# A fourth of the aggregation's seven products is split into seven, in eight of its sixteen units

## The chip, the cores and the metric

The kernel runs on one core of a Trainium2 chip. Time is device microseconds of one execution. Of the core's engines the text speaks of TensorE (PE in the profile, with its weight loads as PEld), VectorE (DVE), ScalarE (ACT), GpSimd (POOL, which here issues large loads) and SyncE (SP, which issues the others).

## The reference, cut to what matters

Two graph layers work on 4096 nodes of 512 features. The part that changes is in the second layer.

```python
# layer 0: x = layernorm(x + relu(adj @ (sign_z(x) @ sign(w0).T)))
# layer 1:
node_att = softmax(x @ node_w, axis=0)
h = x @ edge_w
e = where(adj > 0, h @ h.T, NEG_BIG)
edge_att = softmax(e, axis=1)
output = adj * (node_att * edge_att) @ (x @ weight)
x = layernorm(x + output + bias)
```

The product of the 4096x4096 weights `adj * edge_att` with the 4096x512 features, here called the aggregation, is taken before the product with `weight`, and all of it is float32.

## The kernel before, in words

The kernel has these stages in order: layer 0 (up to 507 us), `h` (507 to 605 us), `h @ h.T` (605 to 1079 us), whose scores go to memory with row maxima and sums, then the aggregation from 1081 to 1911 us, and at last the product with `weight` and the layernorm of the last rows.

**The aggregation's units.** The output's 4096 rows stand in four groups, g = 0 to 3, each of two panels of 512 rows (g and g + 4). The 4096 inputs stand in four pairs of panels as well, r = 0 to 3. A unit (`Aggregate(g, r)`) multiplies one pair of input panels with one pair of output panels and adds to the sums of its group. There are 16 units in the order g, then r, so that units 0 to 3 are group 0, units 4 to 7 group 1, and so on. A unit is a 2x2 block product in the Strassen-Winograd form: seven products m = 0 to 6 instead of eight. The seven left operands come from the features, were made once, and are loaded again for each product from `lop_d` (512 KB). The seven right operands of a unit are its four panels of weights, three of them as they are and one overwritten by a difference, and three more differences (`combine`, `right`). Each is a buffer of 1 MB.

**One product.** Unsplit, a product is two sums (`Sums` with h = 0, 1), each of four matmuls that contract 128 rows, 128x128 weights against 512 columns, into one PSUM bank. Split, which products 6, 4 and 3 are in units 4 to 14, it is a 2x2 block product again: seven products of half the size in each direction, each of two matmuls against 256 columns. They are held in four sums: two small products side by side in a bank for (1, 2), (0, 5) and (3, 4), and one alone for (6,). A sum's life is `seed` (line 1037: ScalarE copies the sum so far into a bank, three sums ahead of use; for the first unit of a group the matmul starts afresh, or VectorE zeroes the bank, line 1039), `multiply` (line 1065) and `evict` (line 1074: ScalarE copies the bank back to memory).

**What splitting costs the other engines.** The small right operands need four 128x512 operations of VectorE for each unit and product (`second`, lines 942 to 946). They are issued from `main`, one half after each unsplit sum. The small left operands need four 128x256 operations for each product and r (`lefts`, lines 955 to 958); these are made in group 0, units 0 to 3, and stored to `lop2_d` through ScalarE's queue. A split product then loads 896 KB in four issues of SP (lines 1049 to 1052) into two of four half-tiles of `lopp`; an unsplit one takes one issue and one half-tile. When a group's last unit has run, seven 128x256 operations for each split product (`join_inner`, line 1113) make its four quarters from the seven small sums, two of them after each sum of products.

**The other work beside it.** While a unit multiplies, the panels of the next one are made: the scores are loaded by POOL (line 810), shifted by the row maximum (VectorE, line 823, 128x2048), exponentiated (ScalarE, line 826), the mask is loaded by POOL (line 817), clipped (ScalarE, line 829), and both are multiplied (VectorE, line 835). Then come the four differences of `combine` (lines 848 to 856). A load waits for a free buffer, and a product frees its right operand's buffer when it ends. After a group, in the next group's first units, come its seven joins (`join`, line 1128, 128x1024 each, held back while inner joins are waiting) and its two finishes (`Finish`): small matmuls with `weight` (line 1192), each read from PSUM by VectorE (line 1203) before the same part of the bank is used again, then the layernorm.

**What sets the order.** The code places the side work by shares of a unit's products (`steps`, `between`), and a scheduler of the framework then fixes one order of instructions for each engine when the kernel is built. Each engine runs its list strictly in order, and waits are semaphores.

The memory `sums` holds two groups in turn (`g % 2`), seven products of 128x1024 for each; small sums that don't fit into their own place lie in two further buffers, `extra`, and so do the small right operands.

Of the kernel before, what the change touches and what calls it, by code (L numbers as in the profile page):

```python
# [21 lines left out]
HUGE = 3.4e38  # L22
TWO = 2.0**11
SHIFT = 1.5 * 2.0**34
SPLIT = 6, 4, 3
WARM = 12


# [1 line left out]
def kernel(  # L30
# [13 lines left out]
    nc = tc.nc  # L44
# [3 lines left out]
    W = 512  # L48
    NG = N // W
    BG = W // P  # L50
    HB = NB // 2
    HG = NG // 2
# [746 lines left out]
    class Aggregate:  # L799
# [114 lines left out]
        def order(self, two):  # L914


            ends = (1, 2) if self.r % 2 else (2, 1)
            if self.last:
                order = 1, 0, 5, 2, 6, 4, 3
            elif two:  # L920
                order = ends[0], 6, 5, 4, 0, 3, ends[1]
            else:
                order = ends[0], 0, 4, 6, 5, 3, ends[1]
            for m in order:
                if two and m in SPLIT:
                    for ns in ((1, 2), (6,), (0, 5), (3, 4)):
                        yield Sums(self, m, ns=ns)
                else:

                    more = bool(self.r) and m == order[0]  # L930
                    keep = self.r < HG - 1 and m == order[-1]
                    for h in range(2):
                        yield Sums(self, m, h, more, keep)

        def second(self, m):

            h, w = BG // 2, W // 2
            r = self.right(m)
            (r11, r12), (r21, r22) = [[r[:, k : k + h, c : c + w] for c in (0, w)] for k in (0, h)]
            t2, t3, t4 = (extra[0][:, n, :].rearrange("p (b w) -> p b w", w=w) for n in range(3))  # L940
            self.halves = r11, r21, r22, t4, r12, t2, t3
            nc.vector.tensor_sub(t3, r22, r12)
            nc.vector.tensor_sub(r12, r12, r11)
            yield
            nc.vector.tensor_sub(t2, r22, r12)
            nc.vector.tensor_sub(t4, r21, t2)
            yield
# [20 lines left out]
        def main(self, between, two):  # L968
            uses = deque(u for u in plan if u.unit is self)
            whole = sum(u.work for u in uses)  # L970
            halves = (None for m in [u.m for u in uses if u.ns and u.ns[0] == 1] for _ in self.second(m))
            stores = deque()
            past = 0
            while plan and plan[0].unit is self:
                u = plan.popleft()
                u.seed()
                u.multiply()
                evict()
                written.append(u)
# [12 lines left out]
                between(past / whole, u.work)  # L992
            if stores:
                next(stores.popleft(), None)
# [13 lines left out]
    class Sums:  # L1008
# [5 lines left out]
        def __init__(self, unit, m, h=0, more=False, keep=False, ns=None):  # L1014
# [4 lines left out]
            self.w = W // 2 * len(ns) if ns else W  # L1019
            self.bank = None  # L1020

        def to(self):

            return part(self.unit.g, self.m, self.ns) if self.ns else sums[:, self.unit.g % 2, self.m, self.h, :]

        def seed(self):


            if self.bank is not None or self.more and not kept:
                return  # L1030
            if self.more:
                self.bank = kept.popleft()
                return
            self.bank = banks.popleft()
            if self.unit.r:
                assert self.ns or not any(m == self.m for m, _ in [*inner, *inner_next])
                nc.scalar.copy(self.bank[:, : self.w], self.to())  # L1037
            elif self.w < W:
                nc.vector.memset(self.bank[:, : self.w], 0.0)

        def multiply(self):
# [12 lines left out]
            if self.ns:  # L1054
                products = []
                for k, n in enumerate(self.ns):
                    at = self.lefts[n]
                    lop = lops["high"][:, at - 4] if at > 3 else lops["low"][:, at]
                    products.append((self.bank[:, ts(k, W // 2)], lop, self.unit.halves[n], BG // 2))
            else:  # L1060
                products = [(self.bank, lops["lop"][:, :, ts(self.h, P)], self.unit.right(m), BG)]
            start = not r and self.w == W
            for ps, lop, rop, K in products:
                for k in range(K):
                    nc.tensor.matmul(ps, lop[:, k, :], rop[:, k, :], start=start, stop=(k == K - 1), skip_group_check=True)  # L1065
# [4 lines left out]
        def evict(self):  # L1070
            u = self.unit
            if not self.keep:
                assert u.r or not self.ns or not any(m == self.m for m, _ in [*inner, *inner_next])
# [24 lines left out]
    def join_inner(g, m, n):  # L1098
# [14 lines left out]
        nc.vector.tensor_add(out_, a, b)  # L1113
# [144 lines left out]
    def in_two(n):  # L1258

        return HG <= n < len(blocks) - 1  # L1260
# [85 lines left out]
    for n, u in enumerate(blocks):  # L1346
# [25 lines left out]
        def between(past, work):  # L1372
            while first and first[0][0] <= past + 1e-6:
                first.popleft()[1]()
            for _ in range(2):
                if inner:
                    join_inner(u.g if u.r else (u.g - 1) % HG, *inner.popleft())
            inner.extend(inner_next)
            inner_next.clear()
            owed[0] += work  # L1380
# [59 lines left out]
```

## Time and profile before

| | us |
|---|---|
| median of 9 runs | 1941.94 |
| lowest and highest | 1939.87, 1947.89 |
| profiled execution, its time | 1944.2 |
| profiled execution, its span | 1942.2 |
| aggregation, units 0 to 15 | from 1081.2 to 1910.9 |
| last finishes | 1910.9 to 1942.2 |

The profile's span is the program's own; 2.0 us of the execution's time lie around it. The granted TensorE clock is 0.998. Units begin at 1277.2 (unit 4), 1328.9, 1387.8, 1440.1 (unit 7), 1487.5, 1539.7, 1596.9, 1651.9 (unit 11), 1700.3, 1751.7, 1808.6 and 1857.7 us (unit 15). The duration of a record is longer than the distance from one to the next, because an engine begins an instruction before the one before has fully ended; both are used below, and the text says which.

| group of instructions, units 4 to 14 | count | busy us | mean ns |
|---|---|---|---|
| seeds by ScalarE, 512 wide (line 1037) | 124 | 73.6 | 599 |
| evictions by ScalarE, 512 wide (line 1074) | 170 | 97.8 | 584 |
| evictions by ScalarE, 256 wide (line 1074) | 33 | 12.3 | 374 |
| reads of the finish by VectorE (line 1203) | 78 | 37.0 | 477 |

### The profile page before, as it was taken

The page shows a single profiled execution, that of the slowest core. Times are in us where ns is not written, and L with a number is a line of the kernel's source. Part 1 is how long each engine was busy: PE and PEld are TensorE (multiplying, and loading weights), DVE is VectorE, ACT ScalarE, POOL GpSimd, SP SyncE. Part 2 cuts the span into 40 slices and gives each one's busy share as a digit, 9 for nine tenths or more (in the row PEclk, how much of TensorE's full clock was granted, in tenths as well). Part 3 has the DMA queues.
Part 4 walks back from the last instruction along what each step waited for, and adds up shares of the span by engine and source line. Part 5 has one row for each costly group of instructions (what it writes and reads, how often), then busy time and mean ns, then how long its engine had stood idle before and what let it go on. Part 6 is the DMA issues. An engine that isn't in the chain of part 4 may idle for free.

```text
span 1942.2 us, 20257 instructions
## 1 busy us (share of the span) xinstructions
PE 1920.4 (99%) x6742; PEld 1203.8 (62%) x6742; DVE 1389.4 (72%) x2062; ACT 1022.2 (53%) x1614; POOL 299.9 (15%) x424
## 2 busy tenths in 40 slices
PE   9999999999999999999999999999999999999998
PEld 6888888888644445454555444456666666666655
DVE  7766676676774566577666787587869987798747
ACT  5433333333202567567667566556766577657731
POOL 0122222222341111111112111111011110111100
PEclk9999999999999999999999999999999999999999
DMA  9888888888475478577769998777778777887731
GB/s 310 298 324 312 292 322 310 320 304 292 146 281 206 175 254 318 185 275 257 282 255 326 330 330 301 254 275 254 265 265 293 255 270 263 287 279 253 272 111 44
DMA packets 171751, 517.11 MB, mean 266 GB/s; under 512 B 15872, under 2 KB 41216, under 8 KB 163968
## 3 DMA queue, kind: packets, MB, share of 16 engines
q1 hardware_dynamic: 89472, 226.39, 34.3%
q0 software_dynamic: 66912, 247.49, 34.3%
q10 hardware_dynamic: 15264, 41.95, 5.9%
q8 instruction: 53, 0.87, 0.2%
q14 instruction: 50, 0.41, 0.1%
HBM read 389.94 MB, written 125.83 MB: 266 GB/s over the span
## 4 chain that ended last, share of the span: by engine, by line
PE 79%; issue 6%; DMA 6%; DVE 6%; ACT 2%; POOL 1%; POOLq 0%; SPq 0%; DVEq 0%; ACTq 0%
PE bank L1065 30%; PE seven L702 12%; PE acc L374 11%; PE acc L373 11%; PE seven L101 4%; PE po L1192 3%; PE pe L633 2%; PE pt L603 2%; DMA s_d<-slot 2%; DMA slot<-s_d 2%; DMA lop<-lop_d 1%; ACT line L574 1%; PE pw L214 1%; PE acc L246 1%; DMA lent<-in_adj_t_dram 1%
## 5 line engine op out<-in xcount | busy, mean ns | idle before, releaser
L1065 PE MATMUL bank<-lent,lop 128*128 128x512 f32 (+1 forms) x1292 | 426.1, 481 | 0.0
L373 PE MATMUL acc<-xw,hi 128*128 128x512 f32 x960 | 376.4, 392 | 0.0
L374 PE MATMUL acc<-xw,lo 128*128 128x512 f32 x960 | 374.2, 390 | 0.0
L1065 PE MATMUL bank<-slot,lop 128*128 128x512 f32 (+1 forms) x896 | 347.1, 535 | 0.7 <-ACT bank L1037 0.7
L1065 PEld LDWEIGHTS bank<-lent,lop 128*128 128x128 f32 x1292 | 246.0, 191 | 154.9 <-issue 133.2
L1065 PEld LDWEIGHTS bank<-slot,lop 128*128 128x128 f32 x896 | 170.0, 190 | 153.8 <-issue 142.3
L363 ACT CAST hi<-at 128x1024 fp32r<-128x1024 f32 x120 | 126.4, 1054 | 203.4 <-PE acc L373 148.4
L365 DVE TENSOR_TENSOR lo<-at,hi 128x1024 fp32r<-128x1024 f32 x120 | 148.0, 1234 | 84.3 <-ACT hi L363 84.3
L374 PEld LDWEIGHTS acc<-xw,lo 128*128 128x128 f32 x960 | 180.4, 188 | 37.0 <-DVE lo L365 0.3
L373 PEld LDWEIGHTS acc<-xw,hi 128*128 128x128 f32 x960 | 180.3, 188 | 36.7
L1074 ACT COPY over<-bank 128x512 f32<-128x512 f32 x200 | 114.8, 581 | 121.0 <-PE bank L1065 111.7
L633 PE MATMUL pe<-hT 128*128 128x512 f32 (+3 forms) x384 | 132.1, 486 | 0.0
L574 ACT ACTIVATE line<-line,nmax_c 128x512 f32<-128x512 f32 x160 | 114.8, 725 | 20.9 <-DVE nmax_c L565 20.8
L565 DVE CUSTOM_DVE_ANT_0 line<-lent,slot 128x512 f32<-128x512 bf16 x144 | 93.1, 688 | 45.2 <-ACT slot L643 22.4
L829 ACT ACTIVATE slot<-slot 128x2048 f32<-128x2048 f32 x40 | 76.5, 1912 | 71.6 <-DMA slot<-in_adj_t_dram 71.4
L823 DVE CUSTOM_DVE_ANT_1 slot<-slot,line 128x2048 f32<-128x2048 f32 x36 | 82.4, 2288 | 36.3 <-DMA slot<-s_d 35.9
L826 ACT ACTIVATE slot<-slot 128x2048 f32<-128x2048 f32 x36 | 68.9, 1913 | 43.0 <-DVE slot L823 42.5
L633 PEld LDWEIGHTS pe<-hT 128*128 128x128 f32 x384 | 64.6, 191 | 41.4 <-issue 33.8
L702 PE MATMUL seven<-hT 128*128 128x512 f32 x192 | 89.8, 593 | 0.0
L1037 ACT COPY bank<-over 128x512 f32<-128x512 f32 x144 | 84.8, 596 | 3.2 <-ACT over L1074 0.4
L603 PEld LDWEIGHTS pt<-ident,lent 128*128 128x128 f32 x412 | 51.2, 141 | 55.2 <-issue 38.8
L604 ACT COPY slot<-pt 128x512 f32<-128x512 f32 (+3 forms) x126 | 69.5, 554 | 27.8 <-PE pt L603 24.0
(260 smaller groups left out, 2864.6 us busy)
## 6 DMA issues: line engine op xcount, KB each, us to landing
at<-in_adj_t_dram SPq DMA_DIRECT2D x60, 1024.0 KB, 6.8
slot<-in_adj_t_dram POOLq DMA_DIRECT2D x42, 1024.0 KB, 6.8
lop<-lop_d SPq DMA_DIRECT2D x79, 512.0 KB, 4.9
slot<-s_d POOLq DMA_DIRECT2D x36, 1024.0 KB, 7.8
s_d<-slot POOLq DMA_DIRECT2D x33, 1024.0 KB, 6.8
lent<-s_d POOLq DMA_DIRECT2D x28, 1024.0 KB, 7.7
lop<-lop_d SPq DMA_DIRECT2D x99, 256.0 KB, 4.4
lent<-in_adj_dram SPq DMA_DIRECT2D x48, 512.0 KB, 5.1
```

What stands on the lines that cost most here:

```text
L363: nc.scalar.copy(hi, aq)
L365: nc.vector.tensor_sub(lo, aq, hi.bitcast(F32))
L373: nc.tensor.matmul(acc, hi[:, c, :], xw[:, kb, :], start=(kb == 0), stop=False)
L374: nc.tensor.matmul(acc, lo[:, c, :], xw[:, kb, :], start=False, stop=(kb == NB - 1))
L565: nc.vector.tensor_tensor_reduce(line, mask, src, -1.0, HUGE, ALU.add, ALU.min, accum_out=nmax_c[:, b, c : c + 1])
L574: nc.scalar.activation(line, line, AF.Exp, bias=nmax_c[:, b, c : c + 1], scale=-1.0, accum_out=sum_c[:, b, c : c + 1])
L603: nc.tensor.transpose(pt[:, j, :], src[:, ts(j, P)], ident)
L633: nc.tensor.matmul(pe[:, lo * P :], hT[:, k, ts(A * BG + i, P)], hT[:, k, (B * BG + lo) * P : (B + 1) * W], start=(k == 0), stop=(k == KD ...
L702: nc.tensor.matmul(ps, left[m][:, k, q, :], right[m][:, k, :], start=(first and k == 0), stop=(k == KD // 2 - 1), skip_group_check=not first,)
L1037: nc.scalar.copy(self.bank[:, : self.w], self.to())
L1065: nc.tensor.matmul(ps, lop[:, k, :], rop[:, k, :], start=start, stop=(k == K - 1), skip_group_check=True)
L1074: nc.scalar.copy(self.to(), self.bank[:, : self.w])
```

## The change

Product 5 is split as well, in the units with two levels that are not the first of their group: units 5, 6, 7, 9, 10, 11, 13 and 14. The first unit of each group still computes it whole, into the sum's own place.

- In these eight units the order of products is now first end, 6, 0, 4, 5, 3, second end, where it was first end, 6, 5, 4, 0, 3, second end. Products 4, 5 and 3, all split, now follow one another.
- The small sums of product 5 lie in the place of product 0 of the other group, and its small right operands in that of products 5 and 6, which are free once the other group's joins are done.
- In the second unit of a group the sums (0, 5) and (6,) begin afresh, since the first unit left a whole product. One operation then subtracts one quarter of that from another (n = 7 in `join_inner`), so that the seven later additions give the right quarters.
- `second` is now issued after the six sums of unsplit products and two of product 5's own, by counts of 1, 1, 2, 2, 1, 1. Those before product 3 are issued while product 5 runs.
- The left operands of product 5 are made in units 1, 2 and 3 and stored with the others.
- `join_inner` makes 28 operations for a group, and one more, where it made 21.

```diff
-SPLIT = 6, 4, 3
+SPLIT = 6, 4, 3, 5
+LATER = 5
@@ order
+            elif two and not self.r:
+                order = ends[0], 6, 5, 4, 0, 3, ends[1]
             elif two:
-                order = ends[0], 6, 5, 4, 0, 3, ends[1]
+                order = ends[0], 6, 0, 4, 5, 3, ends[1]
...
-                if two and m in SPLIT:
+                if two and m in SPLIT and (self.r or m != LATER):
                     for ns in ((1, 2), (6,), (0, 5), (3, 4)):
@@ second
-            t2, t3, t4 = (extra[0][:, n, :].rearrange("p (b w) -> p b w", w=w) for n in range(3))
-            self.halves = r11, r21, r22, t4, r12, t2, t3
+            buf = sums[:, (self.g + 1) % 2, 5:7].rearrange("p m h w -> p (m h) w") if m == LATER else extra[0]
+            t2, t3, t4 = (buf[:, n, :].rearrange("p (b w) -> p b w", w=w) for n in range(3))
+            self.halves[m] = r11, r21, r22, t4, r12, t2, t3
@@ main
-            halves = (None for m in [u.m for u in uses if u.ns and u.ns[0] == 1] for _ in self.second(m))
+            self.halves = {}
+            halves = deque(x for u in uses if u.ns and u.begin for x in [self.second(u.m)] * 2)
+            counts = deque((1, 1, 2, 2, 1, 1) if self.r else (1,) * 6)
...
-                if not u.ns:
-                    next(halves, None)
+                if counts and (not u.ns or u.m == LATER and u.ns[0] in (1, 6)):
+                    for _ in range(min(counts.popleft(), len(halves))):
+                        next(halves.popleft())
...
-                    if not self.g and u.m in SPLIT:
+                    if not self.g and u.m in SPLIT and (self.r or u.m != LATER):
                         stores.append(self.lefts(u.m, lops["lop"]))
@@ Sums
+            self.new = not unit.r or bool(ns) and m == LATER and unit.r == 1 and ns[0] in (0, 6)
...
-            if self.unit.r:
-                assert self.ns or not any(m == self.m for m, _ in [*inner, *inner_next])
+            if not self.new:
+                assert not any(m == self.m for m, *_ in [*inner, *inner_next])
                 nc.scalar.copy(self.bank[:, : self.w], self.to())
...
-            start = not r and self.w == W
+            start = self.new and self.w == W
...
-                inner_next.extend((self.m, n) for n in range(7))
+                inner_next.extend((self.m, n, u.g) for n in range(7))
+            if self.end and self.m == LATER and not u.r and in_two(blocks.index(u)):
+                inner_next.append((self.m, 7, u.g))
@@ part
+        if m == LATER:
+            return sums[:, (g + 1) % 2, 0].rearrange("p h w -> p (h w)")[:, slice(0, 2 * w) if len(ns) == 2 else slice(2 * w, 3 * w)]
@@ join_inner
+        if n == 7:
+            nc.vector.tensor_sub(c12, c12, c22)
+            return
```

More of the change, by code (lines that the diff above doesn't have):

```diff
@@ L1058, in multiply @@
                     lop = lops["high"][:, at - 4] if at > 3 else lops["low"][:, at]
-                    products.append((self.bank[:, ts(k, W // 2)], lop, self.unit.halves[n], BG // 2))
+                    products.append((self.bank[:, ts(k, W // 2)], lop, self.unit.halves[m][n], BG // 2))
             else:
                 products = [(self.bank, lops["lop"][:, :, ts(self.h, P)], self.unit.right(m), BG)]
-            start = not r and self.w == W
+            start = self.new and self.w == W
             for ps, lop, rop, K in products:
@@ L1072, in evict @@
             if not self.keep:
-                assert u.r or not self.ns or not any(m == self.m for m, _ in [*inner, *inner_next])
+                assert u.r or not any(m == self.m or m == LATER and not self.m for m, *_ in [*inner, *inner_next])
                 nc.scalar.copy(self.to(), self.bank[:, : self.w])
@@ L1096, with join_inner @@
     inner, inner_next = deque(), deque()
[L1098 removed]
+    def join_inner(m, n, g):
         w = W // 2
         (c11, c12), (c21, c22) = ((x[:, :w], x[:, w:]) for x in (sums[:, g % 2, m, h, :] for h in range(2)))
+        if n == 7:
+            nc.vector.tensor_sub(c12, c12, c22)
+            return
         both = part(g, m, (0, 5))
@@ L1376, in between @@
                 if inner:
-                    join_inner(u.g if u.r else (u.g - 1) % HG, *inner.popleft())
+                    join_inner(*inner.popleft())
             inner.extend(inner_next)
```

## The prediction

> **What bounds the kernel.** I read the page's head and chain first, then TensorE's own order of time, then who kept TensorE waiting, then each engine's load unit by unit.
>
> ```profile
> span 1942.2 us, 20257 instructions
> PE 1920.4 (99%) x6742; PEld 1203.8 (62%) x6742; DVE 1389.4 (72%) x2062; ACT 1022.2 (53%) x1614; POOL 299.9 (15%) x424
> ...
> PE 79%; issue 6%; DMA 6%; DVE 6%; ACT 2%; POOL 1%; POOLq 0%; SPq 0%; DVEq 0%; ACTq 0%
> ```
>
> TensorE (PE) is busy throughout and carries the chain. A busy TensorE can still hide slack, so its pace has to be read where the change works. This is unit 7 of the aggregation in order of time (start, length, count):
>
> ```profile
> 1448.80 19.12 PE L1065 MATMUL bank<-lent,lop 128*128 128x256 f32 x72
> 1467.75 7.03 PE L1065 MATMUL bank<-slot,lop 128*128 128x512 f32 x16
> 1474.62 6.21 PE L1065 MATMUL bank<-lent,lop 128*128 128x256 f32 x28
> ```
>
> One matmul leaves two records. The second line is one whole product: 16 records in 7.03 us, the last of which counts for its full 592 ns, so the pitch is (7.03 - 0.592) / 15 = 0.429 us. The third is one split product: (6.21 - 0.379) / 27 = 0.216 us. Half the columns take 1.5 ns more than half the time; weight loads, 190 ns each, fit under both. (The first line merges products of both kinds.) The busy sums of the page's groups give 0.442 and 0.235, because the modelled end of one record overlaps the next group; I don't use them.
>
> What TensorE waited for between 1277 and 1858 us, units 4 to 14 (total us, times, longest), is little:
>
> ```profile
> PE po L1192 <- DVE xb L1203: 4.8, 7, 1.1
> PE bank L1065 <- ACT bank L1037: 0.7, 1, 0.7
> ```
>
> So whatever shortens the matmul stream there shortens the kernel, as long as the other engines keep up. Units 7, 8, 11 and 12 by engine (stretch, sum, then busy time of PE, PEld, DVE, ACT, POOL):
>
> ```profile
> 1440.10:1487.50 47.40, 47.40 (x165) 29.91 (x164) 38.20 (x42) 34.28 (x48) 5.99 (x8) 1.00 0.84 296
> 1487.50:1539.70 52.20, 51.05 (x173) 32.59 (x172) 52.07 (x54) 27.91 (x32) 6.73 (x9) 1.00 0.77 267
> ...
> 1651.90:1700.30 48.40, 47.74 (x166) 29.87 (x165) 37.16 (x36) 33.95 (x46) 5.98 (x8) 1.00 0.83 288
> 1700.30:1751.70 51.40, 51.03 (x174) 32.49 (x173) 51.24 (x53) 26.71 (x32) 6.41 (x9) 1.00 0.75 259
> ```
>
> VectorE (DVE) is full in units 8 and 12, where a group's joins fall, and about 80% full in the units before. Its lateness is what TensorE waits for at the end of unit 8:
>
> ```profile
> 1535.41 2.29 DVE L823 CUSTOM_DVE_ANT_1 lent<-lent,line 128x2048 f32<-128x2048 f32 x1
> 1537.62 0.68 DVE L945 TENSOR_TENSOR lent<-slot 128x512 f32<-128x512 f32 x1
> 1538.22 0.48 DVE L1203 SCALAR_TENSOR_TENSOR xb<-po,f,xb 128x256 f32<-128x256 f32 x1
> ...
> 1538.75 1.13 PE L1192 MATMUL po<-over 128*128 128x256 f32 x4 [1.15 <-DVE xb L1203]
> ```
>
> **The change, part by part.** Eight units (5, 6, 7, 9, 10, 11, 13, 14) compute product 5 split.
>
> *Matmuls.* Each of the eight loses 8 matmuls of 512 columns (16 records) and gains 14 of 256 (28 records): 16 x 0.429 = 6.86 us becomes 28 x 0.216 = 6.05 us, 0.82 us saved, 6.5 us for eight. All of it is on the bounding engine. [...] This stage's rows already hold both widths at 0.216 and 0.429 us and decide for the saving.
>
> *VectorE.* A 128x512 operation shows 0.68 us but follows the next at 0.605 us when VectorE is full, a 128x256 one shows 0.42 us and follows at 0.335 us (three joins of line 1113 at 1492.87 take 1.09 us: (1.09 - 0.42) / 2). Added:
> - The right-hand combinations: 4 per unit, 32 x 0.605 = 19.4 us.
> - The inner joins: 7 for each of three groups and one subtraction for each, 24 x 0.335 = 8.0 us, and three zeroings of 0.2 us.
> - The left-hand combinations in units 1, 2 and 3: 12 x 0.335 = 4.0 us, and 6 stores issued from ScalarE's queue. Those units have 7.0, 25.2 and 6.9 us of VectorE idle each, and TensorE doesn't wait there: 0 (at worst, uncovered, 1.3 us in each of two).
>
> Units 4 to 14 have 101 us of VectorE idle in 580, so the average is no problem. The places are. Units with r = 1 or 2 get 2.4 us against 7.8 to 15.7 us of idle: hidden, except where an eviction of the finish (line 1203) comes out later behind other work. Of the present evictions many reach TensorE with 0.1 to 3 us to spare. I put 0.5 us on those of units 4 to 6; those of units 9, 10, 13 and 14 follow waits for panels (6.2 us of VectorE idle in unit 9 alone) that swallow the lag.
>
> At the full unit 8 I counted. In unit 7 VectorE idles 8.84 us before line 763, until TensorE's matmul of line 772 is done; the built order puts product 5's four combinations ahead of that, into the idle time. From line 763 to the eviction at 1538.22 the built order has eight more 128x256 operations and two fewer 128x512: 8 x 0.335 - 2 x 0.605 = +1.5 us. TensorE arrives 0.8 us earlier. Its wait there grows by 2.3 us, and the next one (0.83 us, at 1544) is then already served: +1.5 us. In units 11 to 13 the same count gives 1 to 2 us, but 3.25 us of VectorE's idle time, a wait for a panel at 1679, lies in that stretch: +0.5 us. Together +2.5 us. Bounds: -4.8 (the new order removes today's waits too) and +11.7 (the rival below).
>
> *ScalarE.* 13 copies of 0.58 us and 13 of 0.38 us more, 12.5 us in all or 1.6 us per unit, in units where it is busy 68 to 75%. Seeds are written three sums ahead. The one wait today, 0.7 us at 1696.7, comes from a clip (line 829) that waits 4.61 us for its mask load and stands ahead of the last product's second seed; in the built order of units 7 and 11 that clip comes after both seeds. I take -0.7. Bounds: -0.7, and +4.5, if in each of units 7, 11 and 14 an operation of 1.9 us gets in front of a seed that has about 0.4 us to spare, as one had at 1679.6.
>
> *Loads.* A split product loads 896 KB in four issues instead of 512 KB in one. SP issues 24 more at 0.3 to 0.5 us each; SP itself mostly waits for buffers. With 4, 5 and 3 now in a row and four buffers in turn, the second half-tile of 5 and of 3 can be issued one split product (6.05 us) before its product, and is used 12 records (2.6 us) into it: 8.6 us of lead, where it was 11.5. Such loads land in 4.4 us in the median, the slowest in 8.7 to 9.3. I take +0.3 us, between 0 and +3 (0.7 us short on half of the eight). POOL's panel loads wait for buffers that a product frees; 0 and 5 change places, but a buffer still comes free at the end of each product and the second still lasts 6.86 us, so they keep their times: 0.
>
> Sum: -6.5 + 2.5 - 0.7 + 0.3 = -4.4 us. The profiled execution took 1944.2 us (span 1942.2 and 2.0 around it), 2.3 above the median of 1941.94; it would become 1939.8, and the median 1937.5.
>
> **Rivals.** A difference under 0.2%, 3.9 us, is about what this kernel's times (1939.87 to 1947.89) can't tell from none. The saving stays above that while new waits are under 2.6 us, and the kernel is slower by it from 10.4 us of new waits.
>
> 1. VectorE takes the gain at its full units. In the middle: its lag passes on at half its size in the two full units and at some tight evictions, new waits of about 4.5 us, 1939.9. For: slack of 0.1 to 3 us before many evictions. Against: panel waits that take up lag. Slower: nothing is absorbed. All that a unit with r = 3 and the next one gain (2.4 + 2.3 + 0.3 us) and the 0.8 us by which TensorE comes earlier pass on, 5.9 us at each of the two full units: 11.7 - 6.5 = +5.2, 1947.1. Against: the count above, +1.5 instead of 5.
> 2. ScalarE holds back seeds in the run 4, 5, 3: +4.5 instead of -0.7, and the rest as forecast: 1942.7. For: split products need 4.1 us of copies in 6.05 us, and exponentials of 1.9 us come between. Against: most seeds are 3 us or more ahead, and the clip's new place.
> 3. Late left operands: +3 instead of +0.3, 1940.2. DMA is 75 to 84% busy already.
> 4. The narrow matmuls don't hold 0.216 us with operands in the sums' memory, say 0.235: 224 x 0.019 = 4.3 us back, 1941.8; at 0.245, with the waits, it is slower. Nothing in the rows speaks for it.
> 5. Today's waits (5.5 us) vanish too: -12, 1930.
>
> **Chances.** Forecast 0.45, within 1935.4 (no new waits) to 1938.0. Rival 5, in part, 0.06. Rival 1 in the middle 0.22, slower 0.08. Rival 2 0.09, rival 3 0.06, rival 4 0.04, of which 0.03 slower. So faster 0.51, same 0.38, slower 0.11. The range runs from 1934 to 1944: it leaves out most of rival 5, the slower end of 1 and 4, and little else.
>
> **What would show it.** Right: 1136 records of 512 columns and 1148 of 256 under the product line at 0.429 and 0.216; units 5, 6, 7 and so on shorter by 0.8 us where nothing waits; waits of TensorE for line 1203's evictions near 7 us in total, most of the growth at the end of units 8 and 12; none for seeds in unit 11. Wrong: those waits well over 10 us (rival 1), a wait for the seed copies of several us (rival 2), for left operands (rival 3), or split pitches above 0.216 (rival 4). The forecast errs most easily on the new order of VectorE's work, which decides which eviction stands behind which 2.2 us operation.

## The result, and the profile after

The changed kernel takes 1951.03 us (median of 10 runs, 1947.02 to 1956.09), where the kernel before takes 1942.80 us (median of 32, 1939.87 to 1947.89). The ratio is 1.0042, with a 95% interval from 1.0033 to 1.005: slower by 8.2 us, outside the predicted range of 1934 to 1944. The profiled execution took 1948.07 us, 3.9 us more than the profiled one of before: that one lay 1.4 us above its median and this one 3.0 us below, so the pair of traces holds less than half of the difference.

Line numbers in the rows are each kernel's own; lines 1212, 1223, 1076, 824 and 857 of the changed kernel are 1192, 1203, 1065, 823 and 856 of the kernel before. First the head of the page of the changed kernel, to be held against that of before:

```profile
span 1946.3 us, 20611 instructions
PE 1916.3 (98%) x6838; PEld 1221.8 (63%) x6838; DVE 1422.5 (73%) x2133; ACT 1030.9 (53%) x1640; POOL 300.7 (15%) x424
```

TensorE is busy for 4.1 us less, VectorE for 33.1 us more. Now TensorE in order of time (start, length, count), in unit 7: a split product and a whole one.

```profile
1449.12 6.21 PE L1076 MATMUL bank<-lent,lop 128*128 128x256 f32 x28
1455.16 7.03 PE L1076 MATMUL bank<-slot,lop 128*128 128x512 f32 x16
```

Both lengths are those of before, to the digit. The line of the products has 1136 records of 512 columns and 1148 of 256, as forecast. The saving of the matmuls is therefore there, and unit 7 shows it whole: 46.5 us where it had 47.4. What TensorE waited for in units 4 to 14 (1275 to 1862 us; total us, times, longest):

```profile
PE po L1212 <- DVE xb L1223: 9.7, 8, 2.9
PE bank L1076 <- ACT bank L1048: 3.0, 2, 2.4
PE bank L1076 <- DVE lent L950: 1.2, 1, 1.2
PE bank L1076 <- DMA lop<-lop_d: 0.8, 1, 0.8
```

14.7 us, where it was 5.5. Units 7, 8, 11 and 12 by engine (stretch, sum, busy time of PE, PEld, DVE, ACT, POOL, then clock, DMA share, GB/s):

```profile
1440.50:1487.00 46.50, 46.50 (x177) 32.15 (x176) 38.05 (x45) 34.64 (x51) 5.99 (x8) 1.00 0.87 302
1487.00:1541.20 54.20, 51.30 (x174) 32.55 (x173) 53.56 (x57) 28.23 (x34) 6.73 (x9) 1.00 0.77 269
1653.40:1700.60 47.20, 47.02 (x177) 31.98 (x176) 37.99 (x42) 35.20 (x51) 5.98 (x8) 1.00 0.87 298
1700.60:1754.70 54.10, 50.45 (x169) 31.75 (x168) 51.81 (x57) 28.04 (x34) 6.36 (x9) 1.00 0.73 258
```

Units 7 and 11 are shorter by 0.9 and 1.2 us, units 8 and 12 longer by 2.0 and 2.7. VectorE (third busy time) fills unit 8 still, and not quite unit 12. The wait at the end of unit 8, in order of time:

```profile
1534.27 0.48 DVE L1223 SCALAR_TENSOR_TENSOR xb<-po,f,xb 128x256 f32<-128x256 f32 x1
1534.66 2.28 DVE L857 TENSOR_TENSOR lent<-slot,lent 128x2048 f32<-128x2048 f32 x1
1536.86 0.69 DVE L947 TENSOR_TENSOR lent<-slot 128x512 f32<-128x512 f32 x1
1537.46 2.29 DVE L824 CUSTOM_DVE_ANT_1 lent<-lent,line 128x2048 f32<-128x2048 f32 x1
1539.67 0.48 DVE L1223 SCALAR_TENSOR_TENSOR xb<-po,f,xb 128x256 f32<-128x256 f32 x1
...
1540.20 1.13 PE L1212 MATMUL po<-over 128*128 128x256 f32 x4 [2.90 <-DVE xb L1223]
...
1745.16 1.13 PE L1212 MATMUL po<-line,line 128*128 128x256 f32 x4 [2.48 <-DVE xb L1223]
```

Between the two evictions stand two operations of 2.28 us, the last `combine` and a shift. Before, only the shift stood there (the prediction shows its row, at 1535.41), and the `combine`, then line 856, came ahead of the first eviction:

```profile
1532.22 2.28 DVE L856 TENSOR_TENSOR slot<-lent,lent 128x2048 f32<-128x2048 f32 x1
1534.42 0.48 DVE L1203 SCALAR_TENSOR_TENSOR xb<-po,f,xb 128x256 f32<-128x256 f32 x1
```

VectorE is never idle here; it does other things first. The last line of the rows of after is the like wait at the end of unit 12. The longest wait that isn't for an eviction is in unit 5. A row of VectorE, ScalarE's rows and then TensorE's:

```profile
1358.53 2.29 DVE L824 CUSTOM_DVE_ANT_1 slot<-slot,line 128x2048 f32<-128x2048 f32 x1 [2.33 <-DMA slot<-s_d]
...
1360.86 1.91 ACT L827 ACTIVATE slot<-slot 128x2048 f32<-128x2048 f32 x1 [3.73 <-DVE slot L824]
...
1363.14 1.92 ACT L830 ACTIVATE lent<-lent 128x2048 f32<-128x2048 f32 x1
1365.07 1.28 ACT L1256 ACT_TABLE_LOAD   x1
...
1367.51 0.60 ACT L1048 COPY bank<-over 128x512 f32<-128x512 f32 x1
...
1368.16 3.57 PE L1076 MATMUL bank<-lent,lop 128*128 128x256 f32 x8 [2.41 <-ACT bank L1048]
```

ScalarE waited 3.73 us for a shift of VectorE, and that shift had waited 2.33 us for its scores to land. Then 6.6 us of ScalarE's own work, an exponential and a clip among it, stood ahead of the seed. The last line has a second cost: 8 records of 256 columns take 3.57 us, where 8 such records take 1.89 us elsewhere in this trace. They run at half the clock: the granted clock is 0.50 from 1368.0 to 1371.4 us (more below).

The profiled execution adds up so. From the distances between records, stalls in units 4 to 14 (whatever is beyond the pitch: waits, smaller gaps, and records at half the clock) grew from 7.8 to 21.3 us, +13.5 (units 4 to 6: +4.0; 7 and 8: +2.0; 9, 10 and 14: +2.8; 11 to 13: +4.7); the matmuls save 6.5; the aggregation began 2.5 us earlier than in the execution shown of before, and what follows unit 15 was 0.7 us shorter. 13.5 - 6.5 - 2.5 - 0.7 = +3.8, against 3.9 measured. The earlier start doesn't come from the change: over the twenty traces of this text the aggregation begins anywhere between 1078.7 and 1083.7 us. The aggregation alone, from its first product to the end of its last, took 837.1 us instead of 829.9.

### The profile page after: what moved, and what is told of

Same layout as the page of the kernel before. It is cut to its first block, busy times and chain, and to the rows that moved or that the text cites. A ratio compares the mean times of both kernels' runs of the same rounds, so it can differ in the third digit from the quotient of the medians.

```text
span 1946.3 us, 20611 instructions
## 1 busy us (share of the span) xinstructions
PE 1916.3 (98%) x6838; PEld 1221.8 (63%) x6838; DVE 1422.5 (73%) x2133; ACT 1030.9 (53%) x1640; POOL 300.7 (15%) x424
## 5 line engine op out<-in xcount | busy, mean ns | idle before, releaser
L1076 PE MATMUL bank<-lent,lop 128*128 128x256 f32 (+1 forms) x1212 | 400.4, 479 | 5.4 <-ACT bank L1048 3.0
L1076 PEld LDWEIGHTS bank<-lent,lop 128*128 128x128 f32 x1212 | 230.8, 191 | 148.3 <-issue 122.4
L1076 PEld LDWEIGHTS bank<-slot,lop 128*128 128x128 f32 x976 | 185.0, 190 | 142.6 <-issue 127.0
L1085 ACT COPY over<-bank 128x512 f32<-128x512 f32 x216 | 121.3, 573 | 91.6 <-PE bank L1076 80.9
L1048 ACT COPY bank<-over 128x512 f32<-128x512 f32 (+1 forms) x154 | 89.8, 590 | 5.4 <-DVE over L1133 2.6
L827 ACT ACTIVATE slot<-slot 128x2048 f32<-128x2048 f32 x37 | 70.8, 1913 | 39.4 <-DVE slot L824 38.1
L830 ACT ACTIVATE slot<-slot 128x2048 f32<-128x2048 f32 x28 | 53.6, 1913 | 64.0 <-DMA slot<-in_adj_t_dram 64.0
L830 ACT ACTIVATE lent<-lent 128x2048 f32<-128x2048 f32 x32 | 61.1, 1911 | 49.1 <-DMA lent<-in_adj_t_dram 46.8
```

The source lines that it names most:

```text
L830: nc.scalar.activation(self.a[n], self.a[n], AF.Relu)
```

## The experiments

All times are medians beside runs of the kernel before on the same chip; the difference to those runs is given, for the changed kernel +8.2. The ratios are taken over whole sets of runs and need not be those of the medians.

### VectorE's added work, or the order of products

```diff
# e1_no_joins
-            if self.end and self.ns and (u.r == HG - 1 ...
+            if self.end and self.ns and self.m != LATER and (u.r == HG - 1 ...
-                inner_next.append((self.m, 7, u.g))
# e2_no_right_sums, in second()
+            if m == LATER:
+                self.halves[m] = r11, r21, r22, r11, r12, r21, r22
+                yield
+                yield
+                return
# e3_neither: both
# e4_order_alone, in the kernel before
+            elif two and self.r:
+                order = ends[0], 6, 0, 4, 5, 3, ends[1]
```

> Leaves out of the changed kernel the seven inner joins of product 5 in three groups and the three subtractions that go with them (24 operations of 128x256 on VectorE, 8 us by the 0.335 us row), so product 5 is not put together at the end. Matmuls, copies, loads and the order of products stay. Theory V (VectorE's added work makes it late, and TensorE waits for it, directly at line 1223's evictions and indirectly through ScalarE's seeds): the waits at 1540 and 1745 us of the changed kernel's profile (3.06 and 2.64 us), which lie behind these joins, fall to 1.5 us or less each, and the time to 1945 to 1948, against 1951.0 of the changed kernel. Theory O (the new order, with three split products in a row, makes ScalarE and the loads late, whatever VectorE does): 1950 to 1952, with the waits of units 5 and 9 unchanged.

> Leaves out of the changed kernel product 5's four right-hand combinations in each of eight units (32 operations of 128x512 on VectorE, 19.4 us); the raw quarters of the right-hand panel are used in their place, so product 5's value is not the reference's. The joins stay. Theory V: most of the lateness in units 5, 9 and 13 goes, the seed wait of 2.58 us at 1368 with it, and the wait at 1745 shrinks; 1943 to 1946. If the joins alone were the cause, 1949 to 1951. Theory O: 1950 to 1952.

> Leaves out both the joins and the subtractions of product 5 and its right-hand combinations, so that VectorE has the load of the kernel before but for the left-hand combinations of three early units; TensorE's matmuls, ScalarE's copies, the loads and the order of products are the changed kernel's. The output is not the reference's. Theory V: what is left is the saving of the matmuls, 6.5 us: 1935 to 1938, and TensorE's waits in units 4 to 14 are about 5 us as before. Theory O: these waits remain at some 12 us, and the time is 1947 to 1951.

> The kernel before with the changed kernel's order of products alone (0 third, 5 fifth) in the units after the first of each group; product 5 is not split. Theory V: as before, 1941 to 1944. Theory O: slower by most of what the change lost besides its saving of 6.5 us, so 1947 to 1955.

| | median us | to before | ratio, 95% interval |
|---|---|---|---|
| e1, without joins | 1950.78 | +8.3 | 1.0036 (1.0023 to 1.0049) |
| e2, without right-hand combinations | 1950.27 | +7.8 | 1.0042 (1.0030 to 1.0054) |
| e3, without both | 1948.18 | +5.7 | 1.0031 (1.0020 to 1.0042) |
| e4, new order alone | 1946.24 | +3.8 | 1.0015 (1.0005 to 1.0025) |

Theory V falls as it stood: 27 us of VectorE's work taken out bring 2.5 us, and the saving of 6.5 us stays away. Theory O is nearer: e1, e2 and e3 lie in its ranges, though for the order alone it began at 1947, a little too high. Yet most of the waits are still for VectorE. The order alone, which adds no operation to any engine, has this at the end of unit 8:

```profile
1536.44 0.47 DVE L1205 SCALAR_TENSOR_TENSOR xb<-po,f,xb 128x256 f32<-128x256 f32 x1
...
1538.88 2.28 DVE L823 CUSTOM_DVE_ANT_1 lent<-lent,line 128x2048 f32<-128x2048 f32 x1
1541.09 0.48 DVE L1205 SCALAR_TENSOR_TENSOR xb<-po,f,xb 128x256 f32<-128x256 f32 x1
...
1541.62 2.07 PE L1194 MATMUL po<-over 128*128 128x256 f32 x4 [3.25 <-DVE xb L1205]
```

Up to this eviction VectorE has one shift more since the start of the unit than in the kernel before (six, where it has five): the scheduler wrote VectorE's list anew, and other rows of the trace show the same (one 128x2048 operation moved from unit 9 to unit 8, a shift from unit 12 to 13). The wait is 3.25 us where it was 1.15, and the four records behind it take 2.07 us instead of 1.13, at about half the pace.

### Long operations, pinned shifts, and an exchange of two split products

```diff
# f1_halved (changed kernel) and f4_before_halved: shift, weigh and combine
-            pinned[0](nc.vector._custom_dve(TENSOR_ADD_SAT, out=q, in0=q, in1=m, ...))
+            for k in (slice(0, 2), slice(2, 4)):
+                pinned[0](nc.vector._custom_dve(TENSOR_ADD_SAT, out=q[:, k], in0=q[:, k], in1=m[:, k], ...))
# f2_pinned_shift (changed kernel)
-            pinned[0](nc.vector._custom_dve(TENSOR_ADD_SAT, ...
+            tc.keep_in_program_order(nc.vector._custom_dve(TENSOR_ADD_SAT, ...
# f3_swap_6_3_4 (kernel before)
-                order = ends[0], 6, 5, 4, 0, 3, ends[1]
+                order = ends[0], 6, 5, 3, 0, 4, ends[1]
```

> The changed kernel with VectorE's long operations (shift, mask product and the four differences of the panels, 128x2048, 2.28 us each) issued as two halves of 1.14 us; nothing is left out, and some 0.03 us are added for each. Theory Q (the loss is that an eviction or a combination which TensorE waits for stands behind a 2.28 us operation in VectorE's list): the waits of TensorE for line 1223's evictions halve, from 9.7 to about 5 us in units 4 to 14, and the time falls to 1944 to 1948. Theory S (the loss lies in what a split product asks of ScalarE and of the loads, and VectorE only shows it): 1950 to 1953.

> The changed kernel with each shift (line 824) held behind everything that the code issued on VectorE before it, where the scheduler lets the shifts of the unit after next go ahead of the finish's evictions. Nothing is left out. Theory Q: the waits at the ends of units 8 and 12 shrink to 1 us or less, unless the shifts come too late for their unit; 1943 to 1948. Theory S: 1950 to 1953.

> The kernel before with two split products, 4 and 3, in each other's place in the two-level units; the work of every engine and the places of split and unsplit products stay as they were. It is an edit with no cost of its own. Theory R (every edit makes the scheduler write VectorE's list anew, the list of before has fewer long operations ahead of evictions than a typical one, and the loss of 3.8 us that the new order alone showed is of that kind): 1944 to 1948, with waits at other places. Theory P (the place of product 5 behind 4 is what costs): 1941 to 1944, as before.

> The kernel before with the same halving of VectorE's long operations as in the changed kernel's run of this set. Theory Q: its 5.5 us of waits in units 4 to 14 fall to about 3, so 1939 to 1942. Theory S: as before or slower by the added 0.03 us for each, 1942 to 1945.

Measured: f1 1951.05 (+8.7), f2 1947.70 (+5.4, its runs from 1940.13 to 1959.19), f3 1943.12 (+0.8; ratio 1.0003, 0.9994 to 1.0012), f4 1948.96 (+6.6; 1.0030, 1.0018 to 1.0042). Theory Q in its simple form falls: halves don't help, the changed kernel still waits 11.0 us for evictions in the profiled run, and the kernel before loses 6.6 us by them. Theory S has f1 in its range, but not f4 (1942 to 1945). Pinning the shifts helps by some 3 us, with a large spread. Theory R in its widest form falls too: the exchange of 3 and 4 costs nothing, as theory P had it. In its trace VectorE has, unit by unit, the same numbers of operations of each kind as before in units 4 to 13. So not every edit costs. The new order alone (e4), which does cost, moved long operations between units; that the moves are its cause is not shown.

### Copies, loads, and the joins on GpSimd

```diff
# g1_no_copies: on top of e3
+            self.new = not unit.r or bool(ns) and m == LATER
...
+                if self.m != LATER or not self.ns:
                     nc.scalar.copy(self.to(), self.bank[:, : self.w])
# g2_raw_left: on top of e3
+            if self.begin and (not self.ns or m == LATER):
                 lops["lop"] = lopp.tile([P, BG, HD], F32, name="lop")
# g3_both: both
# g4_pool_joins (changed kernel, complete)
-            todo.extend(lambda g=u.g, n=n: join(g, n, nc.vector) for n in range(7))
+            todo.extend(lambda g=u.g, n=n: join(g, n, nc.gpsimd) for n in range(7))
```

> The run without joins and right-hand combinations, in which also ScalarE's copies of product 5's small sums are left out (32 evictions and 26 seeds; the sums start afresh in each of the eight units), so that ScalarE has less to do than in the kernel before. Matmuls, loads and the order of products stay. That run took 1948.2 us where the saving of the matmuls alone would give 1936. Theory A (ScalarE's copies, dense in the run of products 4, 5, 3, hold TensorE back): 1938 to 1942. Theory L (the loads of the small left operands do): 1947 to 1950. Theory N (neither: the units' other work sets the pace once TensorE is faster, by whatever stands ahead in VectorE's list): 1945 to 1949.

> The run without joins and right-hand combinations, in which also product 5's small left operands are not loaded or made: one load of 512 KB as for an unsplit product, and its raw quarters used for the seven small matmul pairs. Copies stay. Theory L: 1938 to 1942. Theory A: 1947 to 1950. Theory N: 1945 to 1949.

> Both of this set's omissions in one kernel: of the split of product 5 only the matmuls, and the new order of products, remain. Theories A and L: 1937 to 1940, the order's own loss of 3.8 us and the saving of 6.5 us. Theory N: 1943 to 1947; the saving of the matmuls turns into waits even with nothing added.

> The changed kernel, complete, with the seven outer joins of a group (128x1024, 1.14 us each on VectorE) done by GpSimd, which takes longer for each but is idle 85% of the time. VectorE loses 8 us of work in units 4 and 5, 8 and 9, 12 and 13, and the finishes start later. Theory V (VectorE's fullness in units 8 and 12 is what TensorE waits for): the waits at their ends go, 1944 to 1948. Theory Q (what stands directly ahead of an eviction decides, not the load): 1948 to 1953, with waits at other places.

Measured: g1 1952.65 (+9.9), g2 1945.01 (+2.3), g3 1949.62 (+6.9), g4 2000.70 (+58). Theory A falls: without 58 of ScalarE's copies the kernel is 4.2 us slower than with them (+9.9 against +5.7). In g1's trace no wait for a seed is left in units 4 to 14, but 10.4 us of waits for evictions and 2.7 us for right-hand combinations are. Leaving out the loads gains about 3 us in both pairs (e3 to g2, g1 to g3), less than theory L wants, and what is left in g3, the matmuls and the order, is still slower than before. That is theory N, though it was too low for g1 and g3, which lie 3.7 and 2.6 us above its ranges. Theories V and Q both missed g4. The GpSimd joins took 3.3 us each, where VectorE takes 1.2, and the products that wait for the joins' memory came 6.2 to 6.6 us late in units 4, 8 and 12; that run says little of VectorE's fullness. Three kernels that differ in these omissions show one wait at the end of unit 8. First e3, then g1, TensorE in order of time:

```profile
1543.91 1.42 PE L1215 MATMUL po<-over 128*128 128x256 f32 x4 [2.40 <-DVE xb L1226]
```

```profile
1544.13 1.13 PE L1216 MATMUL po<-over 128*128 128x256 f32 x4 [2.40 <-DVE xb L1227]
```

2.40 us in both (and in g3), with ScalarE's copies and without. In all three the same four operations of VectorE, two shifts of 2.28 us and two combinations of 0.68 us, stand between the two evictions there, without a gap: the length of the wait comes from what stands in VectorE's list.

### Room on VectorE, the old order, a slower pace

```diff
# h1_after_no_outer, h2_before_no_outer
-            todo.extend(lambda g=u.g, n=n: join(g, n, nc.vector) for n in range(7))
+            todo.extend([lambda: None] * 7)
# h3_split_old_order (changed kernel)
-                order = ends[0], 6, 0, 4, 5, 3, ends[1]
+                order = ends[0], 6, 5, 4, 0, 3, ends[1]
-            counts = deque((1, 1, 2, 2, 1, 1) if self.r else (1,) * 6)
+            counts = deque((2, 2, 1, 1, 1, 1) if self.r else (1,) * 6)
# h4_after_pace65 (changed kernel)
-            while owed[0] >= 6:
-                owed[0] -= 6
+            while owed[0] >= 6.5:
+                owed[0] -= 6.5
```

> The changed kernel without the seven outer joins of the first three groups (21 operations of 128x1024 on VectorE, 1.14 us each, 8 us in each of units 4, 8 and 12 with their neighbours); seven empty steps keep their place in time. The output leaves those joins out. Theory 1 (no room on VectorE in units 8 and 12): TensorE's waits at the ends of these units go, and this kernel is as fast as the kernel before without the same joins or faster, up to the 6.5 us of the matmuls: 1936 to 1941. Theory 2 (the order of products): its loss of some 4 us stays, 1945 to 1949.

> The kernel before without the same outer joins, as the base for the run above. Theory 1: its few waits in units 8, 9 and 12 (about 4 us) go, 1938 to 1941. Theory 2: 1940 to 1943.

> The changed kernel with product 5 split but left in its old place, third, ahead of 4 and 0, in all two-level units; its right-hand combinations come during the first product. Complete. Theory 2: about 4 us faster than the changed kernel, 1944 to 1948. Theory 1: VectorE's work in units 7, 8, 11 and 12 is the same, so 1948 to 1954.

> The changed kernel with the steps of joins and finishes issued after every 6.5 units of matmul work instead of 6, so that the same work of VectorE lies over more units. Complete. Theory 1: less of it in units 8 and 12, shorter waits there, 1944 to 1949. Theory 2: the order's loss stays, 1949 to 1952.

Measured: h1 1958.86 (+16.0; ratio 1.0088, 1.0073 to 1.0102), h2 1950.12 (+7.2; 1.0037, 1.0025 to 1.0049), h3 1951.77 (+8.9), h4 1952.40 (+9.5). Both theories fall. Without 24 us of VectorE's work both kernels are slower by 7 to 8 us. The trace of h2, VectorE and then TensorE at the end of unit 12, shows how that can be:

```profile
1721.88 2.29 DVE L823 CUSTOM_DVE_ANT_1 slot<-slot,line 128x2048 f32<-128x2048 f32 x1 [3.67 <-DMA slot<-s_d]
...
1729.13 2.29 DVE L835 TENSOR_TENSOR lent<-lent,slot 128x2048 f32<-128x2048 f32 x1 [1.98 <-ACT lent L826]
...
1735.04 2.28 DVE L835 TENSOR_TENSOR slot<-slot,slot 128x2048 f32<-128x2048 f32 x1
...
1737.85 2.28 DVE L850 TENSOR_TENSOR lent<-lent,slot 128x2048 f32<-128x2048 f32 x1
...
1740.65 2.28 DVE L853 TENSOR_TENSOR lent<-lent,lent 128x2048 f32<-128x2048 f32 x1
1742.85 0.48 DVE L1203 SCALAR_TENSOR_TENSOR xb<-po,f,xb 128x256 f32<-128x256 f32 x1
...
1734.67 1.03 PE L1192 MATMUL po<-over 128*128 128x256 f32 x4
...
1743.38 2.07 PE L1192 MATMUL po<-line,line 128*128 128x256 f32 x4 [4.27 <-DVE xb L1203]
```

The sums that the eviction at 1742.85 reads were done by 1735.7. VectorE had idled in this unit, for a panel and for ScalarE, because its list has those operations first; then three operations of 2.28 us (lines 835 at 1735.04, 850 and 853) stood ahead of the eviction, and TensorE waited 4.27 us. With less to do, VectorE had a worse order. That the change costs 8.7 us in this pair too (h1 to h2) speaks against the joins as its cause. The old order (h3) brings no gain with the split, and the slower pace none.

### The same lists, other loads

```diff
# i1_after_packed, i2_before_packed: left operands kept as [P, 7, 2, BG, P]
-                nc.sync.dma_start(low[:, :2].rearrange("p n b f -> p (n b) f"), raw[:, :, :P])
+                nc.sync.dma_start(low[:, :2].rearrange("p n b f -> p (n b) f"), raw[:, 0])
...
-                nc.sync.dma_start(high[:, 2], raw[:, BG // 2 :, P:])
+                nc.sync.dma_start(high[:, 2], raw[:, 1, BG // 2 :])
```

> The changed kernel, complete, with the left operands kept in memory with the two halves of a product's 256 columns apart, so that a small left operand is read in pieces of 1 and 2 KB instead of 512 bytes. Bytes, issues and the order of instructions on every engine in the aggregation stay; the packets of 512 bytes (9.5% of the 16 engines' time in units 4 to 14 of the changed kernel) go, and the same 15.7 MB take about 7.5%. Layer 0 writes the operands in shorter pieces. Theory D (the loads' share of the DMA engines decides how late the panels are, and with them VectorE): waits shrink, 1944 to 1948. Theory R (the lists alone): 1949 to 1953.

> The kernel before with the same layout of the left operands. Theory D: a gain as well, smaller, since its units leave more room on the DMA engines: 1939 to 1942. Theory R: 1941 to 1944.

Measured: i1 1952.25 (+10.7; ratio 1.0048, 1.0036 to 1.0060), i2 1942.27 (+0.7; 1.0003, 0.9994 to 1.0012). Theory D falls, theory R holds, though the test was weaker than written: the packets of 512 bytes moved 17.9 bytes per ns and DMA engine, those of 1 and 2 KB some 21, so that they took 9.4% of the engines' time and their successors 8.2%, not 7.5%. The lists of TensorE, VectorE and ScalarE are the same, instruction for instruction, in i1 and the changed kernel, and in i2 and the kernel before. What the pair does show is how closely the waits belong to the lists. TensorE's waits in units 4 to 14 of i1, and its two long waits for evictions in order of time:

```profile
PE po L1212 <- DVE xb L1223: 12.7, 9, 2.9
PE bank L1076 <- ACT bank L1048: 2.1, 1, 2.1
PE bank L1076 <- DVE lent L950: 1.7, 1, 1.7
```

```profile
1541.05 1.13 PE L1212 MATMUL po<-over 128*128 128x256 f32 x4 [2.90 <-DVE xb L1223]
...
1746.38 1.13 PE L1212 MATMUL po<-line,line 128*128 128x256 f32 x4 [2.48 <-DVE xb L1223]
```

2.90 and 2.48 us, as in the changed kernel, to the digit, in another execution with other packets. The seed wait of unit 5 is there too (2.1 us). These two waits are no accident of one run: the order of instructions brought them both times.

**All traces together.** TensorE's time in units 4 to 14 can be parted in each of the twenty traces into stalls, counted from the pitch as above, and the rest. The rest is 572.5 us in each of the six kernels that compute product 5 whole, and 564 to 568 us in the fourteen that split it: the saving of the matmuls is in all of them. The stalls are 6 to 15 us in the six and 16 to 28 us in the fourteen (71 with the joins on GpSimd), whatever else was left out or moved. In g3, which keeps only the matmuls of the split and the new order, they are 20 us, where the order alone (e4) has 10. In each of the fourteen the stalls thus grew by at least 8 us over the kernel before, which has 8, and that is more than the matmuls save. A single unlucky list doesn't account for it.

## Why the prediction was wrong

**The premise.** "Whatever shortens the matmul stream there shortens the kernel" rested on the chain of the whole span, 79% TensorE, and on how little TensorE waited. Read for units 4 to 14 alone, the chain of the kernel before says something else. Its pieces in order of time (start, length, what), shown only from 1620 to 1740 us:

```profile
1620.54 7.55 DMA lent<-in_adj_t_dram
1628.12 1.92 ACT lent L829
...
1645.55 0.74 POOL lent L810
...
1668.26 10.88 DMA slot<-s_d
...
1679.25 2.29 DVE slot L823
...
1736.79 2.29 DVE slot L848
1739.07 0.41 DVE xb L1203
1739.52 1.13 PE po L1192 x4
```

From 1613.4 to 1739.5 us, the end of unit 10, unit 11 and most of unit 12, the chain has no TensorE in it. It goes through the making of the panels: a buffer comes free, POOL issues a load, the load takes 7.6 to 10.9 us, ScalarE and VectorE work on it, and VectorE reaches the eviction that TensorE waits for (0.37 us, at 1739.5). Added up over units 4 to 14, TensorE has 377 of the chain's 581 us (65%); with the new order alone (e4) 276 of 583, without VectorE's added work (e3) 187 of 588, without the loads as well (g2) 174 of 587. (The rest is VectorE, loads, and time for which the profile shows no releaser, much of it ahead of POOL's issues. Releasers are inferred, so these are readings and not measurements.) The reading that fits is that two chains of nearly the same length ran side by side; the change shortened one, and the other set the pace. The shares don't prove it, for they don't follow the loss: TensorE has 307 and 333 us of the chain in f3 and i2, which lose nothing, but 352 in g3, 357 in h2 and 374 in f4, which lose 6.6 to 7.2 us. One wait of 0.37 us is enough to give 126 us of the chain to other engines, at a time when TensorE was busy almost throughout. In the changed kernel the chain could be followed back to 1722 us only; it begins there in the making of the panels:

```profile
1722.43 10.69 DMA lent<-in_adj_t_dram
1733.14 1.92 ACT lent L830
1735.08 2.29 DVE slot L836
```

Step by step:

- **Matmuls, -6.5: right.** Pitches, lengths and counts as forecast; rival 4 is out.
- **VectorE, +2.5: this is the step that failed.** In its place the profile has +6.1 us: waits for evictions grew by 4.9 us (4.8 to 9.7), and one for a right-hand combination (1.2) came. They are larger than the term although most of VectorE's added work is hidden. For unit 8, the one counted instruction by instruction, +1.5 was forecast together with the next wait, and stalls in units 8 and 9 grew by 1.8. But 0.5 us each for units 4 to 6 and 11 to 13, and nothing for 10 and 14, became 4.0, 4.7 and 3.0 us of stalls by all causes. The term had been worked out as a sum of added work. The runs show that leaving the work out hardly helps (27 us of work, 2.5 us of time), so a sum of work was the wrong measure. At the ends of units 8 and 12 the rows show what made the waits: which operations stand between two evictions in VectorE's list, which is new with nearly every edit. That this order makes the whole loss is argued, not shown; in unit 5 it began with a load that landed late.
- **ScalarE, -0.7: wrong in sign, within its bounds.** Waits for seeds grew from 0.7 to 3.0 us, 2.4 of them in unit 5. Rival 2 had it right that exponentials would get in front of a seed, but not what follows: they were late because a shift came late from VectorE, and without ScalarE's added copies (g1) the waits for seeds are gone and the time is longer all the same.
- **Loads, +0.3: near, as far as TensorE waits for them** (0.8 us). Their part in the panels' chain was left out: without product 5's small loads the time falls by 3 us in both pairs, with lists that changed as well. Which of the two it is stays open.
- **The clock was not in the sum.** The granted clock over all runs averages 0.9987 in the kernel before (88 runs) and 0.9975 in the changed one (11). TensorE is busy for 98% of the span, so the lost share is about the lost time, an estimate: 0.0013 x 1940 = 2.5 and 0.0025 x 1949 = 4.9 us. The difference, 2.4 us, is nearly a third of the 8.2. It isn't a cause beside the waits: in unit 5 the clock of 0.50 comes behind a wait of 2.41 us, and the table below has half pace behind all 11 stalls of 3.2 us and more.
- **Rival 1** came closest, in its slower end: TensorE's gain turned into waits, 1947.1 at a chance of 0.08. Its half-way middle, 1939.9, had 0.22. New waits of 10.4 us, the point that I named for slower, were nearly reached by the profile's waits (14.7 - 5.5 = 9.2 us) and passed by the stalls (+13.5 us), which hold smaller gaps and the records at half the clock as well. That the waits come without VectorE's added work (e3, g3) the rival did not have.

**What stays open.** No run holds the split together with VectorE's list of before, so what makes the stalls is not settled: that they come with the split is shown for fourteen lists, that the shorter matmul stream meets a second chain is the reading that fits best. As it is the change costs 8.2 us; with three edits made to both kernels it cost 2.1 (halved operations, 8.7 against 6.6), 8.7 (no outer joins) and 10.0 us (packed loads, 10.7 against 0.7): it never paid. No version tried is faster than the kernel before.

## What to carry to other kernels

Read the chain for the stage that the change touches, not for the span: where it leaves the bounding engine for long stretches, a second chain of about the same length may be there, and a saving on the first may turn into waits (here 6.5 us of matmuls saved, and 13.5 us more of stalls). How long those stretches are didn't tell how much was lost here. Where a scheduler writes each engine's list, cost an edit by the new list at every place where an engine is full, and don't expect less work to mean less time (with 24 us less of VectorE's work both kernels were slower by 7 to 8 us). Several short waits can cost less than one long one of the same sum: 2 of 68 stalls of 1 to 2 us were followed by half pace, and all 11 of 3.2 us and more (next section).

## What the runs showed of the hardware

A long wait of TensorE can cost more than its length: behind the 2.41 us of unit 5 in the changed kernel eight records took 1.68 us longer (3.57 us, not 1.89). In all 20 traces the stalls of 1 us and more after 1200 us were counted, with the pace of the matmuls behind them (a stall is the distance to the next record beyond the pitch):

| stall | how many | followed by half pace |
|---|---|---|
| 1 to 2 us | 68 | 2, both closely behind a stall of over 6 us |
| 2.0 to 3.1 us | 37 | 12 |
| 3.2 to 6.7 us | 11 | 11 |

Half pace means records of 0.43 us for 256 columns (in the changed kernel, with a granted clock of 0.50 from 1368.0 to 1371.4 us) and 0.85 us for 512 (in the kernel before, with 0.50 from 1082.2 to 1085.6 us), for about 3.4 us; it costs 0.6 to 1.7 us on top of the stall. This is the row of e3 behind its 2.40 us wait, eight records of 512 columns that take 5.05 us instead of 3.60, where g1 after the same wait has none:

```profile
1545.12 5.05 PE L1081 MATMUL bank<-lent,lop 128*128 128x512 f32 x8
```

The kernel before has no stall over 1.31 us in units 4 to 14; the changed one has three over 2.5 us, of which the one in unit 5 led to half pace. In all 20 traces each of the 11 stalls of 3.2 us and more led to it, and so did a third of those between 2.0 and 3.1 us (12 of 37). There the same wait may or may not (2.40 us in e3 and in g1); what decides it is not shown.
